# Two float32 products with 32 outputs on column quarters of TensorE, in place of depthwise products on 64x64 quarters

## The chip, the cores and the metric

The kernel runs on one core of one Trainium2 chip. The metric is the device time of the whole kernel in microseconds. In the profile, PE is TensorE's matmuls and PEld its weight loads, DVE is VectorE, ACT is ScalarE, POOL is GpSimd and SP is SyncE. A float32 matmul of the program stands in the trace as two records of PE and two of PEld, here called passes; a bf16 matmul is one of each.

## What is computed

The input x is 32 images of 96 channels, 56 x 56 pixels, float32. Two residual layers follow each other, each on the group-normalised input (`_gn`, 32 groups of three channels):

```
x = x + L0(gn(x))     # L0: 1x1 conv 96->576, BN, 4-bit activation;
                      #     3x3 depthwise conv on 576, BN, 4-bit activation;
                      #     1x1 conv 576->96, BN; plus its own input
x = x + L1(gn(x))     # L1, on three parts of 32 channels:
                      #   x_0 : 3x3 conv 32->32, weights gated per image
                      #   x_05: fractional Fourier transform (2D), 64x64 channel mix
                      #         gated per image, inverse transform, absolute value
                      #   x_1 : rfft2, 64x64 channel mix gated per image, irfft2
                      #   then a 3x3 conv 96->96 over the three results
```

The weights of L0 are quantised to 4 bits, so its weights and activations are small whole numbers, held exactly in bf16. L1 is computed in float32.

## The kernel before

**The loop.** Every image stays in SBUF as `x` (96 partitions x 3136). Layer 0 of image i and layer 1 of image i-1 are two lists of steps (lines 270 and 349), which `interleave` (line 76) merges in proportion to their lengths: 31 steps of layer 0 with 66 of layer 1. The tile framework then orders the instructions of each engine by this list and by its own estimate of when operands are ready, so that a few products move past others. Every engine works through its queue in that order.

**Layer 0** (lines 270 to 346) cuts an image into 8 chunks of 7 rows (392 pixels).

- `expand(j)` (282): VectorE normalises the chunk (v, line 285), TensorE multiplies it by w1 in five blocks of 128 hidden channels (pe, 288; the last block holds its 64 channels twice), and `quant_act` (257) makes 4-bit values: ScalarE Relu (260), VectorE twice (261, 265), into the padded bf16 planes q1.
- `depthwise(p, b)` (294): a depthwise 3x3 convolution as nine products with diagonal matrices. A diagonal of 64 channels is 64x64, so four products run side by side on the array's four 64x64 quarters: two halves of the block (h, rows) times two chunks of pixels (e, columns). The last block of 64 channels serves four chunks at once, in every second pair of chunks (line 341). Then `quant_act` into q2.
- `project(p)` (320): 72 paired products an image with w3 (pp, 324), then the residual (334) and the statistics for layer 1 (335).

In the list, five expands come first and the other three are put among the first depthwise steps (lines 338 to 345).

**Layer 1** (lines 349 to 609): `norm` (353) makes the statistics (helper `group_stats`, 237: pm, pv on TensorE, VectorE between), xs and x0p, and two DMAs on the SP queue copy x0p shifted by a row up and down, so that three rows of the spatial convolution lie on 96 partitions. Then come 7 transposes (pt, 439), the gates (pg, po; 374 to 384), forward_w (pf, 487), reflect (pr, 455), eight pairs of forward_h (pu, 497) and mix_f (pm, 515; it reads u, which VectorE and ScalarE make in lines 503 to 505), and:

- `mix_t` (558), 7 steps, one for each chunk of 8 rows (448 pixels): one float32 product with the gated weights g2, 128 inputs and 32 outputs (px, 560), for the first chunk a second one that adds the bias (564), and a copy into `cat` on VectorE (565);
- inverse_h (pi, 531), and `spatial` (567), 7 steps: three float32 products for dx = 0, 1, 2 with g0, 96 inputs and 32 outputs, into PSUM partitions 64 to 95 (ps, 570), and an activation into `cat` on ScalarE (578);
- inverse_w (pz, 544), `magnitude` (ScalarE, 553), `final` (580), the 3x3 convolution over `cat` as nine products for each of 7 chunks (pc, 584), and the store.

PSUM has two pools of four banks: ps0 for layer 0 (pe, pd, pp), ps1 for layer 1.

Of the kernel before, what the change touches and what calls it, by code (L numbers as in the profile page):

```python
# [44 lines left out]
NB = 5  # L46
NG64 = 9
# [18 lines left out]
NC0 = 8  # L66
CR0 = H // NC0
CN0 = CR0 * W
# [20 lines left out]
def block_kernel(ctx: ExitStack, tc: tile.TileContext, out: bass.AP, a: dict):  # L89
# [12 lines left out]
    def bank(pool, name):  # L102
        return pool.tile([128, 512], F32, tag="bank", name=name)
# [21 lines left out]
    with tc.tile_pool(name="prep", bufs=1) as pp:  # L125

        def load_tmp(name):
            src = a[name]
            t = pp.tile(list(src.shape), F32, tag=name, name=name)
            nc.scalar.dma_start(out=t, in_=src)  # L130
            return t
# [17 lines left out]
        quantise(w1, C, NB * 128, "1")  # L149
# [3 lines left out]
        quantise(w3f, 128, NG64 * C, "3")  # L153
        w3 = cp.tile([128, NG64 * C], BF16, tag="w3q", name="w3q")
# [4 lines left out]

        ident2 = pp.tile([128, 64], BF16, tag="ident2", name="ident2")  # L160
        nc.vector.tensor_tensor(ident2, ident[:, 0:64], ident[:, 64:128], ALU.add)
        dw = []
        for b in range(NB):
            d = cp.tile([128, 9, 64], BF16, tag=f"dw{b}", name=f"dw{b}")
            for t in range(9):
                nc.vector.tensor_scalar(d[:, t, :], ident2, w2[:, b * 9 + t : b * 9 + t + 1], None, ALU.mult)
            dw.append(d)
# [3 lines left out]
        v9 = load_tmp("vec9")  # L171
# [17 lines left out]
        A2, B2 = batchnorm(v9, 128, 0, NG64, "2")  # L189
# [67 lines left out]
    def quant_act(ps, k, scale, offset, dst, name):  # L257

        t = p4.tile([128, CN0], F32, tag="qt", name=f"qt{name}")
        nc.scalar.activation(t[:k], ps, AF.Relu, bias=offset, scale=scale)  # L260
        nc.vector.tensor_scalar(t[:k], t[:k], 15.0, MAGIC, ALU.min, ALU.add)  # L261
        src = t[:k]
        if len(dst.shape) == 3:
            src = src.rearrange("p (h w) -> p h w", w=W)
        nc.vector.tensor_scalar(dst, src, MAGIC, None, ALU.subtract)  # L265
# [4 lines left out]
    def layer0(i):  # L270
        xt = xts[i]
        s = {}

        def norm():
            stats = p2.tile([C, NCH, 6], F32, tag="bn", name=f"bn{i}")
            for j in range(NCH):
                nc.vector.bn_stats(stats[:, j, :], xt[:, j * CN : (j + 1) * CN])
            mean, rstd, _ = group_stats(stats.rearrange("p c s -> p (c s)"), f"a{i}")
            s["mean"], s["rstd"] = mean, rstd
            stats2[i] = p2.tile([C, NC0, 6], F32, tag="bn2", name=f"bn2{i}")  # L280

        def expand(j):
            part = xt[:, j * CN0 : (j + 1) * CN0]
            v = p2.tile([C, CN0], F32, tag="v", name=f"v{i}_{j}")
            nc.vector.tensor_scalar(v, part, s["mean"], s["rstd"], ALU.subtract, ALU.mult)
            for b in range(NB):
                ps = bank(ps0, f"pe{i}_{j}_{b}")
                nc.tensor.matmul(ps[:, :CN0], w1[:, 128 * b : 128 * (b + 1)], v, start=True, stop=True)  # L288
                dst = q1[b][:, 1 + CR0 * j : 1 + CR0 * (j + 1), 1 : 1 + W]
                quant_act(ps[:, :CN0], 128, A1[:, b : b + 1], B1[:, b : b + 1], dst, f"e{i}_{j}_{b}")  # L290

            nc.vector.scalar_tensor_tensor(part, part, B3, v, ALU.add, ALU.add)

        def depthwise(p, b):


            if b == 0:
                s["q2"] = s.pop("q2n", None) or p2.tile([128, NG64, CN0], BF16, tag="q2", name=f"q2_{i}_{p}")
            if b == NB - 1:
                s["q2n"] = p2.tile([128, NG64, CN0], BF16, tag="q2", name=f"q2_{i}_{p + 1}")  # L300
            pd = [bank(ps0, f"pd{i}_{p}_{b}_{h}") for h in range(2)]
            for t in range(9):
                dy, dx = divmod(t, 3)
                for h in range(2):
                    for e in range(2):
                        j = 2 * p + e + (2 * h if b == NB - 1 else 0)
                        nc.tensor.matmul(  # L307
                            pd[h][64 * e : 64 * e + 64, :CN0],
                            dw[b][64 * h : 64 * h + 64, t, :],
                            q1[b][64 * h : 64 * h + 64, CR0 * j + dy : CR0 * j + dy + CR0, dx : dx + W],  # L310
                            start=(t == 0),
                            stop=(t == 8),
                        )
            for h in range(2):
                g, q2 = (2 * b + h, s["q2"]) if b < NB - 1 else (NG64 - 1, s["q2n"] if h else s["q2"])
                quant_act(
                    pd[h][:, :CN0], 128, A2[:, g : g + 1], B2[:, g : g + 1], q2[:, g, :], f"d{i}_{p}_{b}_{h}"
                )

        def project(p):  # L320
            pp_ = [bank(ps0, f"pp{i}_{p}_{e}") for e in range(2)]
            for g in range(NG64):
                for e in range(2):
                    nc.tensor.matmul(  # L324
                        pp_[e][:C, :CN0],
                        w3[64 * e : 64 * e + 64, g * C : (g + 1) * C],
                        s["q2"][64 * e : 64 * e + 64, g, :],
                        start=(g == 0),
                        stop=(g == NG64 - 1),
                    )  # L330
            for e in range(2):
                j = 2 * p + e
                part = xt[:, j * CN0 : (j + 1) * CN0]
                nc.vector.scalar_tensor_tensor(part, pp_[e][:C, :CN0], A3, part, ALU.mult, ALU.add)
                nc.vector.bn_stats(stats2[i][:, j, :], part)

        ex = lambda j: (lambda: expand(j))
        steps = [norm] + [ex(j) for j in range(5)]
        for p in range(NC0 // 2):

            for b in range(NB - p % 2):
                steps.append(lambda p=p, b=b: depthwise(p, b))
                if (p, b) in ((0, 1), (0, 3), (1, 1)):
                    steps.append(ex({(0, 1): 5, (0, 3): 6, (1, 1): 7}[p, b]))
            steps.append(lambda p=p: project(p))
        return steps


    def layer1(i):
# [205 lines left out]
        def rows(j):  # L555
            return slice(1 + CR * j, 1 + CR * (j + 1))

        def mix_t(j):
            ps = bank(ps1, f"px{i}_{j}")
            nc.tensor.matmul(  # L560
                ps[:G, :CN], s["g2"], s["xs"][:, CR * j : CR * (j + 1), :], start=True, stop=(j > 0)
            )
            if j == 0:
                nc.tensor.matmul(ps[:G, :CN], bias2, pat, start=False, stop=True)
            nc.vector.tensor_copy(cat[:G, rows(j), 1 : 1 + W], ps[:G, :CN].rearrange("p (h w) -> p h w", w=W))

        def spatial(j):
            ps = bank(ps1, f"ps{i}_{j}")
            for dx in range(3):
                nc.tensor.matmul(  # L570
                    ps[2 * G : C, :CN],
                    s["g0"][:, G * dx : G * (dx + 1)],
                    x0p[:, CR * j : CR * (j + 1), dx : dx + W],
                    start=(dx == 0),
                    stop=(dx == 2),
                )
            src = ps[2 * G : C, :CN].rearrange("p (h w) -> p h w", w=W)
            nc.scalar.activation(cat[2 * G : C, rows(j), 1 : 1 + W], src, AF.Identity, bias=b0[2 * G : C], scale=1.0)  # L578
# [19 lines left out]
        def each(f, n):  # L598
            return [lambda k=k: f(k) for k in range(n)]
# [6 lines left out]
        steps += each(mix_t, NCH)  # L606
        steps += each(inverse_h, 4) + each(spatial, NCH) + each(inverse_w, 4) + [magnitude]
# [98 lines left out]
def _layout(inputs):  # L706
# [8 lines left out]
    def hidden(v):  # L715

        p = np.concatenate([v, v[HID - 64 :]])
        return np.moveaxis(p.reshape((NB, 128) + v.shape[1:]), 0, 1)

    def hidden64(v):  # L720

        p = np.moveaxis(v.reshape((NG64, 64) + v.shape[1:]), 0, 1)
        return np.concatenate([p, p])

    k["x"] = np.asarray(inputs["x"])
    w1 = g0("w1")[:, perm, 0, 0].T
    k["w1"] = np.concatenate([w1, w1[:, HID - 64 :]], axis=1)
    k["w2"] = hidden(g0("w2").reshape(HID, 9)).reshape(128, NB * 9)
    k["w3"] = hidden64(g0("w3")[perm, :, 0, 0].T).reshape(128, NG64 * C)
    names = ("b", "g", "be", "m", "v")  # L730
    k["vec576"] = np.stack([hidden(g0(n + "1")) for n in names], axis=1).reshape(128, 5 * NB)
    k["vec9"] = np.stack([hidden64(g0(n + "2")) for n in names], axis=1).reshape(128, 5 * NG64)
# [41 lines left out]
    k["b0"] = np.tile(g1("conv0_b"), 3)[:, None]  # L774
# [21 lines left out]
```

## Time and profile before

| | us |
|---|---|
| time, median of 2 runs (6797.88 and 6801.83) | 6799.85 |
| time of the profiled execution | 6797.88 |
| its span, first to last instruction | 6796.1 |
| mean granted clock of TensorE in it | 0.919 |
| PE busy (92% of the span) | 6275.5 |
| DVE busy (55%) | 3745.0 |
| ACT busy (38%) | 2558.7 |

The page's largest groups of TensorE (busy time, records): pc 1626.3 us in 4032, pe 1164.0 in 2560, pd 1048.2 in 20736, ps 538.7 in 1344, pr 357.1 in 2688, pp 224.6 in 2304, px 200.6 in 448 and 30.7 for its bias. Busy time is a union, so products that run side by side count once. Matmuls are pipelined: the time of one record on the page is longer than the distance of its start from the next one's, and distances are what adds up to the span.

### The profile page before, as it was taken

To read this page: it belongs to the slowest core of one execution; us is meant where nothing else is said; L and a number is where in the kernel's file an instruction comes from. 1 tells how busy PE (TensorE), PEld (TensorE's weight loads), DVE (VectorE), ACT (ScalarE), POOL (GpSimd) and SP (SyncE) were. 2 spreads that over 40 slices of the span, in tenths; PEclk is the share of its full clock that TensorE was granted. 3 is DMA by queue.
4 is the path that set the end of the run, shared out by engine and by line. 5 is a ranking of instruction groups with operands and counts; after the bars stand their busy time and mean duration, and the time that the engine had idled before them with its cause. 6 is when DMAs were issued, how large, how long until landed. Compare 5 with 4: busy or idle time off the path is not lost.

```text
span 6796.1 us, 114554 instructions
## 1 busy us (share of the span) xinstructions
PE 6275.5 (92%) x49088; PEld 3597.5 (53%) x49088; DVE 3745.0 (55%) x9182; ACT 2558.7 (38%) x4488; POOL 80.4 (1%) x114
## 2 busy tenths in 40 slices
PE   6999999999999999999999999999999999999998
PEld 3555555555555555455554555554555545555555
DVE  8466544565446665456654466544566544665442
ACT  4343333433334433344333343333443333433331
POOL 1000000000000000000000000000000000000000
PEclk9999999988999999999999999999999999999997
DMA  1000000000000000000000000000000000000000
GB/s 39 1 20 20 20 20 9 12 20 20 20 8 13 20 20 20 20 1 20 20 20 20 3 18 20 20 20 20 1 20 20 20 20 1 20 20 20 13 13 8
DMA packets 15982, 112.49 MB, mean 17 GB/s; under 512 B 6357, under 2 KB 6927, under 8 KB 7280
## 3 DMA queue, kind: packets, MB, share of 16 engines
q1 hardware_dynamic: 12288, 103.22, 6.8%
q8 instruction: 384, 6.29, 0.4%
q10 hardware_dynamic: 3184, 1.95, 0.1%
q14 instruction: 126, 1.03, 0.0%
HBM read 40.48 MB, written 38.54 MB: 12 GB/s over the span
## 4 chain that ended last, share of the span: by engine, by line
PE 76%; DVE 15%; ACT 7%; issue 1%; POOL 0%; DMA 0%; ACTq 0%; POOLq 0%; DVEq 0%
PE pc L584 24%; PE pe L288 14%; PE pd L307 10%; PE ps L570 8%; PE pr L455 5%; DVE q L265 4%; PE pi L531 3%; PE pm L515 2%; PE px L560 2%; DVE qte L261 2%; PE pp L324 2%; ACT cat L553 2%; ACT u L505 2%; ACT qte L260 2%; PE pu L497 2%; DVE u L504 1%
## 5 line engine op out<-in xcount | busy, mean ns | idle before, releaser
L584 PE MATMUL pc<-cat,wc 96*96 96x448 f32 x4032 | 1626.3, 563 | 102.1 <-ACT cat L553 102.1
L260 ACT ACTIVATE qte<-pe,o,s 128x392 f32<-128x392 f32 x1280 | 839.2, 677 | 1160.2 <-PE pe L288 1060.2
L260 ACT ACTIVATE qtd<-pd,o,s 128x392 f32<-128x392 f32 x1152 | 721.4, 674 | 1360.9 <-PE pd L307 1349.9
L288 PE MATMUL pe<-v,w 96*128 96x392 f32 x2560 | 1164.0, 608 | 54.2 <-DVE gtb L248 43.7
L584 PEld LDWEIGHTS pc<-cat,wc 96*96 96x96 f32 x4032 | 673.4, 170 | 1002.6 <-issue 888.3
L261 DVE TENSOR_SCALAR qtd<-qtd 128x392 f32<-128x392 f32 x1152 | 411.0, 359 | 1238.3 <-ACT qtd L260 1237.2
L307 PE MATMUL pd<-q,dw 64*64 64x392 bf16 x20736 | 1048.2, 339 | 0.6 <-ACT qte L260 0.3
L592 DVE SCALAR_TENSOR_TENSOR x<-pc,bc,x 96x448 f32<-96x448 f32 x224 | 152.3, 680 | 1286.7 <-PE pc L584 1286.7
L307 PEld LDWEIGHTS <-dw 64*64 64x64 bf16 x20736 | 649.8, 108 | 343.9 <-issue 161.0
L288 PEld LDWEIGHTS pe<-v,w 96*128 96x128 f32 x2560 | 570.3, 234 | 462.4 <-issue 238.6
L265 DVE TENSOR_SCALAR q<-qte 128x392 bf16<-128x392 f32 x1280 | 681.6, 555 | 10.9
L570 PE MATMUL ps<-x0p,g 96*32 96x448 f32 x1344 | 538.7, 549 | 0.0
L261 DVE TENSOR_SCALAR qte<-qte 128x392 f32<-128x392 f32 x1280 | 431.8, 355 | 92.2 <-ACT qte L260 84.2
L515 PE MATMUL pm<-g,u 128*57 128x64 f32 x3648 | 263.2, 225 | 199.1 <-ACT u L505 199.1
L265 DVE TENSOR_SCALAR q<-qtd 128x392 bf16<-128x392 f32 x1152 | 410.9, 359 | 25.7
L515 PEld LDWEIGHTS pm<-g,u 128*57 128x57 f32 x3648 | 226.7, 133 | 306.8 <-ACT u L505 289.5
L455 PEld LDWEIGHTS pr<-rev,X 56*128 56x128 f32 x2688 | 343.3, 206 | 38.1 <-DVE qte L261 17.1
L455 PE MATMUL pr<-rev,X 56*128 56x56 f32 x2688 | 357.1, 293 | 0.0
L570 PEld LDWEIGHTS ps<-x0p,g 96*32 96x32 f32 x1344 | 138.0, 110 | 330.5 <-issue 328.4
L505 ACT COPY u<-pu 32x456 f32<-32x456 f32 (+1 forms) x256 | 124.3, 486 | 439.9 <-DVE u L504 366.6
L467 ACT COPY xs<-pr 32x336 f32<-32x336 f32 (+3 forms) x448 | 183.1, 428 | 249.5 <-PE pr L455 135.1
L578 ACT ACTIVATE cat<-ps,b 32x448 f32<-32x448 f32 x224 | 140.6, 627 | 335.1 <-PE ps L570 335.1
(127 smaller groups left out, 5236.1 us busy)
## 6 DMA issues: line engine op xcount, KB each, us to landing
x<-in_x_dram SPq DMA_DIRECT2D x96, 392.0 KB, 5.4
out_dram<-x SPq DMA_DIRECT2D x96, 392.0 KB, 5.8
x0p<-x0p SPq DMA_DIRECT2D x64, 398.8 KB, 5.0
w<-in_w_dram ACTq DMA_DIRECT2D x1, 432.0 KB
wc<-in_wc_dram ACTq DMA_DIRECT2D x1, 324.0 KB
w<-in_w_dram ACTq DMA_DIRECT2D x1, 240.0 KB
cw<-in_cw_dram ACTq DMA_DIRECT2D x1, 128.0 KB
coef<-in_coef_dram ACTq DMA_DIRECT2D x1, 128.0 KB
```

What stands on the lines that cost most here:

```text
L260: nc.scalar.activation(t[:k], ps, AF.Relu, bias=offset, scale=scale)
L261: nc.vector.tensor_scalar(t[:k], t[:k], 15.0, MAGIC, ALU.min, ALU.add)
L265: nc.vector.tensor_scalar(dst, src, MAGIC, None, ALU.subtract)
L288: nc.tensor.matmul(ps[:, :CN0], w1[:, 128 * b : 128 * (b + 1)], v, start=True, stop=True)
L307: nc.tensor.matmul(pd[h][64 * e : 64 * e + 64, :CN0], dw[b][64 * h : 64 * h + 64, t, :], q1[b][64 * h : 64 * h + 64, CR0 * j + dy : CR0 * ...
L455: nc.tensor.matmul(ps[:, W * k : W * (k + 1)], lhs, rev[:, W * kind : W * (kind + 1)], start=True, stop=True)
L467: nc.scalar.copy(o, src)
L505: nc.scalar.copy(u[96:128, :n, :], U[:G])
L515: nc.tensor.matmul(ps[:L, 64 * k : 64 * k + 64], s["u"][:, k, :], s["g1"], start=True, stop=True)
L531: nc.tensor.matmul(ps[: 2 * L, H * k : H * (k + 1)], lhs, e57, start=True, stop=True)
L570: nc.tensor.matmul(ps[2 * G : C, :CN], s["g0"][:, G * dx : G * (dx + 1)], x0p[:, CR * j : CR * (j + 1), dx : dx + W], start=(dx == 0), sto ...
L584: nc.tensor.matmul(ps[:C, :CN], wc[:, C * t : C * (t + 1)], cat[:, CR * j + dy : CR * j + dy + CR, dx : dx + W], start=(t == 0), stop=(t = ...
```

## The change

Layer 0 goes over to 7 chunks of 8 rows, as in layer 1. The depthwise diagonals are 128x128 (64x64 in the last block), one product of 448 pixels after the other; the last block is no longer held twice; each chunk is projected with five products. The list of layer 0 becomes: norm, expand(0), and for each chunk j expand(j+1), five depthwise steps, project(j): 50 steps, merged with 56 of layer 1. In layer 1, `mix_t` and `spatial` take four chunks (the second time three) in one step: chunk e of the group goes to column quarter e of the array, that is, to PSUM partitions 32e to 32e+31 of one bank. The sums, the copies into `cat` and their number are the same.

```diff
-NC0 = 8
-CR0 = H // NC0
-CN0 = CR0 * W
+def blk(b):
+    return 128 if b < NB - 1 else HID - 128 * (NB - 1)
...
-            d = cp.tile([128, 9, 64], BF16, tag=f"dw{b}", name=f"dw{b}")
+            k = blk(b)
+            d = cp.tile([128, 9, 128], BF16, tag=f"dw{b}", name=f"dw{b}")
             for t in range(9):
-                nc.vector.tensor_scalar(d[:, t, :], ident2, w2[:, b * 9 + t : b * 9 + t + 1], None, ALU.mult)
+                nc.vector.tensor_scalar(d[:k, t, :k], ident[:k, :k], w2[:k, b * 9 + t : b * 9 + t + 1], None, ALU.mult)
...
-                nc.tensor.matmul(ps[:, :CN0], w1[:, 128 * b : 128 * (b + 1)], v, start=True, stop=True)
+                nc.tensor.matmul(ps[:k, :CN], w1[:, 128 * b : 128 * b + k], v, start=True, stop=True)
...
-        def depthwise(p, b):
...
-            pd = [bank(ps0, f"pd{i}_{p}_{b}_{h}") for h in range(2)]
+        def depthwise(j, b):
...
+            ps = bank(ps0, f"pd{i}_{j}_{b}")
             for t in range(9):
                 dy, dx = divmod(t, 3)
-                for h in range(2):
-                    for e in range(2):
-                        j = 2 * p + e + (2 * h if b == NB - 1 else 0)
-                        nc.tensor.matmul(
-                            pd[h][64 * e : 64 * e + 64, :CN0],
-                            dw[b][64 * h : 64 * h + 64, t, :],
-                            q1[b][64 * h : 64 * h + 64, CR0 * j + dy : CR0 * j + dy + CR0, dx : dx + W],
-                            start=(t == 0),
-                            stop=(t == 8),
-                        )
+                nc.tensor.matmul(
+                    ps[:k, :CN],
+                    dw[b][:k, t, :k],
+                    q1[b][:k, CR * j + dy : CR * j + dy + CR, dx : dx + W],
+                    start=(t == 0),
+                    stop=(t == 8),
                 )
...
+        def project(j):
+            ps = bank(ps0, f"pp{i}_{j}")
+            for b in range(NB):
+                k = blk(b)
+                nc.tensor.matmul(
+                    ps[:C, :CN], w3[:k, b * C : (b + 1) * C], s["q2"][:k, b, :], start=(b == 0), stop=(b == NB - 1)
+                )
...
+        steps = [norm, lambda: expand(0)]
+        for j in range(NCH):
+            if j + 1 < NCH:
+                steps.append(lambda j=j: expand(j + 1))
+            for b in range(NB):
+                steps.append(lambda j=j, b=b: depthwise(j, b))
+            steps.append(lambda j=j: project(j))
...
-        def mix_t(j):
-            ps = bank(ps1, f"px{i}_{j}")
-            nc.tensor.matmul(
-                ps[:G, :CN], s["g2"], s["xs"][:, CR * j : CR * (j + 1), :], start=True, stop=(j > 0)
-            )
-            if j == 0:
+        def mix_t(a):
+            ps = bank(ps1, f"px{i}_{a}")
+            quarters = [(e, 4 * a + e, ps[G * e : G * (e + 1), :CN]) for e in range(min(4, NCH - 4 * a))]
+            for e, j, o in quarters:
+                nc.tensor.matmul(o, s["g2"], s["xs"][:, CR * j : CR * (j + 1), :], start=True, stop=(j > 0))
+            if a == 0:
                 nc.tensor.matmul(ps[:G, :CN], bias2, pat, start=False, stop=True)
...
-        def spatial(j):
-            ps = bank(ps1, f"ps{i}_{j}")
+        def spatial(a):
+            ps = bank(ps1, f"ps{i}_{a}")
+            quarters = [(e, 4 * a + e, ps[G * e : G * (e + 1), :CN]) for e in range(min(4, NCH - 4 * a))]
             for dx in range(3):
-                nc.tensor.matmul(
-                    ps[2 * G : C, :CN],
-                    s["g0"][:, G * dx : G * (dx + 1)],
-                    x0p[:, CR * j : CR * (j + 1), dx : dx + W],
-                    start=(dx == 0),
-                    stop=(dx == 2),
+                for e, j, o in quarters:
+                    nc.tensor.matmul(
+                        o,
+                        s["g0"][:, G * dx : G * (dx + 1)],
+                        x0p[:, CR * j : CR * (j + 1), dx : dx + W],
+                        start=(dx == 0),
+                        stop=(dx == 2),
+                    )
...
-        steps += each(mix_t, NCH)
-        steps += each(inverse_h, 4) + each(spatial, NCH) + each(inverse_w, 4) + [magnitude]
+        steps += each(mix_t, 2)
+        steps += each(inverse_h, 4) + each(spatial, 2) + each(inverse_w, 4) + [magnitude]
```

The tensors on the host follow: w1 is 576 columns wide where it was 640, w3 480 where it was 864, the second batch normalisation shares the table of the first, and the spatial bias b0 is repeated four times. The evacuations of `mix_t` and `spatial` go over the quarters one by one, on the same engines as before.

## The prediction

> **What bounds the kernel now.** I read the page first: busy time, the clock row, the chain that ended last.
>
> ```profile
> span 6796.1 us, 114554 instructions
> ...
> PE 6275.5 (92%) x49088; PEld 3597.5 (53%) x49088; DVE 3745.0 (55%) x9182; ACT 2558.7 (38%) x4488; POOL 80.4 (1%) x114
> ...
> PEclk9999999988999999999999999999999999999997
> ...
> PE 76%; DVE 15%; ACT 7%; issue 1%; POOL 0%; DMA 0%; ACTq 0%; POOLq 0%; DVEq 0%
> ```
>
> PE holds 76% of the chain and is busy 92% of the span; no other engine passes 55%. The clock is below full almost everywhere. The first matmul (pma) of successive images starts 208.2 us apart, so I work on one image, 3071.7 to 3279.9 us, cut into stages in the view of windows: start, middle (reflections, forward, frequency mix), mix and inverse, spatial, final convolution.
>
> ```profile
> 3071.70:3110.70 39.00, 34.42 (x195) 20.44 (x194) 33.40 (x88) 21.03 (x37) 1.41 (x2) 0.82 0.38 84
> 3110.70:3167.50 56.80, 50.88 (x619) 39.14 (x617) 50.03 (x118) 31.16 (x60) 0.00 (x0) 0.94 0.01 2
> 3167.50:3191.10 23.60, 23.48 (x243) 13.69 (x242) 13.02 (x33) 7.26 (x12) 0.00 (x0) 0.93 0.00 1
> 3191.10:3225.00 33.90, 30.82 (x292) 14.15 (x291) 8.78 (x25) 16.54 (x25) 0.41 (x1) 0.99 0.00 1
> 3225.00:3279.90 54.90, 54.86 (x193) 23.67 (x194) 10.65 (x23) 3.74 (x6) 0.00 (x0) 0.95 0.00 0
> sum 208.20, PE 194.46 PEld 111.09 DVE 115.88 ACT 79.74 POOL 1.81; mean PE 38.89 PEld 22.22 DVE 23.18 ACT 15.95 POOL 0.36
> ```
>
> After each stage's length come PE, PEld, DVE, ACT and POOL busy, then the clock. PE idles 208.2 - 194.5 = 13.7 us. The clock takes, stage by stage, 39.0 x 0.18 + 56.8 x 0.06 + 23.6 x 0.07 + 33.9 x 0.01 + 54.9 x 0.05 = 15.2 us. PE work at full clock is the rest, 179.3 us. So 29 us of an image are idle time and slow clock: a change of order can give them back. In the first two stages VectorE is busy 83.4 of 95.8 us, near to being the bound.
>
> The timeline of PE gives the durations (start, time, what):
>
> ```profile
> 3191.11 2.44 PE L570 MATMUL ps<-x0p,g 96*32 96x448 f32 x6
> 3193.48 1.71 PE L307 MATMUL pd<-q,dw 64*64 64x392 bf16 x36
> 3195.11 4.70 PE L570 MATMUL ps<-x0p,g 96*32 96x448 f32 x12
> ...
> 3225.04 16.64 PE L584 MATMUL pc<-cat,wc 96*96 96x448 f32 x36 [3.12 <-ACT cat L553]
> 3241.61 0.85 PE L307 MATMUL pd<-q,dw 64*64 64x392 bf16 x13
> 3242.40 13.77 PE L584 MATMUL pc<-cat,wc 96*96 96x448 f32 x36
> ```
>
> A float32 matmul is two records (passes). 36 passes of the final convolution take 13.7 us, 381 ns each; the spatial product, with 32 of 128 columns in use, pays 395. One depthwise step (36 products, four at a time on the 64x64 quarters) takes 1.63 us. After 3.12 us of idleness 36 passes take 16.64 us.
>
> **What the Trainium skill says.** "TensorE: Matmul & The Clock Gate", Part 1: idle windows of about 3.4 us halve the clock. The trace agrees and shows more: a stretch without a gap, of small float32 products that wait for weight loads (reflections), halves it too (length, PE, clock):
>
> ```profile
> 3118.20:3121.60 3.40, 3.40 (x33) 1.00 0.00 0
> 3121.60:3128.40 6.80, 6.80 (x16) 0.50 0.00 0
> ```
>
> The same page, "Back-to-back issue gap", prices an N-column pass at N/2.4 + 2.5 ns. Part 3 there gives 2.38x for three column tiles and says that matmuls start in strict order. That matters: if the second pass of quarter 0 held back the first pass of quarter 1, only two passes would overlap. The trace contradicts it:
>
> ```profile
> 3110.50 0.41 PE L487 MATMUL pf<-e57t,X 56*56 56x57 f32 x4
> 3110.70 0.36 PE L307 MATMUL pd<-q,dw 64*64 64x392 bf16 x3
> 3110.75 0.26 PE L487 MATMUL pf<-e57t,X 56*56 56x57 f32 x2
> ```
>
> pf (56x56) fills the first 64x64 quarter and all of it is issued ahead of pd, yet three pd products start on the other quarters before its last two passes. Each tile of the array takes its own next instruction, so I expect four wide. "TensorEngine Tiling (Array Packing)", Key Properties: a change of tiling mode drains the array; the trace shows some 0.1 us at each (395 against 381 ns over six passes).
>
> **The change, PE work of one image at full clock.**
> - Depthwise: 4.5 x 4 = 18 steps of 1.64 us = 29.5 us go. 7 chunks x 5 blocks x 9 taps = 315 products of 448 bf16 columns come, the last block's 64x64 alone on the array. The trace has none of this form. Below: 189 ns by the page's price. Above: 182 ns x 448/392 = 208 ns, from the four-wide step with its four issues. I take 194: 187 ns plus the 7 ns by which a final pass exceeds 448 x 2 / 2.4 = 373. 61.1 us, **+31.6** (bounds +30.0 to +36.0). Weight loads (120 ns at most for 128 float32 columns, from the packed loads of the inverse) stay hidden under 194.
> - Spatial: 42 passes, 16.2 us by the timeline, become two groups of 6 slots: 12 x 0.40 + 0.2 = 5.0. **-11.2** (0 if serial).
> - Fourier mix: 14 passes and 2 for the bias, 6.7 us, become 4 + 2 slots (the bias follows in quarter 0 alone): 2.7. **-4.0**.
> - Expand: 80 passes of 392 columns at 334 ns become 70 of 448 at 381: 26.7 for 26.7. Project: 72 paired products, 6.5 us, become 35 at 194 ns: **+0.3**.
> - Mode changes: from 70 to 91 an image, as the small 64x64-mode products no longer share a mode with the depthwise ones: 21 x 0.1, part of it priced above: **+1.5**.
>
> Sum: 179.3 + 18.2 = **197.5 us**.
>
> *Idle time and clock.* Layer 0 goes from 31 coarse steps to 50, against 56 of layer 1, so a step of 1.7 us stands between nearly all small ones. In the new order pm has 10 to 19 depthwise products ahead of it where it now waits 5.9 us an image for u (ScalarE): 3 left. The final convolution waits 3.12 us for the magnitudes, after 2.7 us of cover; two blocks and a projection (5.4 us) come to stand there: 1 left. The gates' wait of 1.7: 0.5. The start keeps its 2.6 us, and gains: the last projection now comes just before the statistics, whose two VectorE operations (0.58 + 0.51 us, a little more at 448 columns) are no longer under a convolution, +1.3; the transposes wait for xs behind five products where eleven ran, +1. Sum 9.4, from 13.7. Slow clock: of five slow stretches (one of 3.4 us, four of 6.8) those at the gates, the reflections (now every other step dense) and the convolution should go; the start's stays (3.4 us lost), the inverse's half: 4.3, from 15.2.
>
> An image: 197.5 + 9.4 + 4.3 = **211.2 us**, +3.0; 31 images in the steady state: +93. The ends cancel roughly: the first image's layer 0, alone, has 94 us of PE work where it takes 81 now (+15 with its waits); the last image's layer 1, alone, saves what the two products cost there (10.1 + 19.0 to some 10, -19). 6796 + 93 is 6889 against the profiled execution's span; its time is 6797.9, the median 6799.9, so 2 to 4 us more: **6890**.
>
> What I cost at nothing: ScalarE gets the four spatial evacuations (627 ns each) in a burst after a bank is full, with expand's activations queued behind; a whole expand (3.8 us) on four other banks covers them, at most 2 us an image if not. VectorE's seven copies of the mix stay (606 ns). The x0p copies (SP queue, 5 us) are issued in the norm, 110 us ahead of their use; loads and stores keep their places. VectorE's layer 0 work is about the same, spread more evenly.
>
> **Rivals.**
> 1. *Two passes at a time* (order, or the moving data of four float32 streams; the trace has only two bf16 streams per row). Spatial takes 8.7 and mix 4.6: +5.6 an image, 7065. Against it: the pf/pd order above.
> 2. *The losses are not returned* (the slower side): a chunk's expand, five depthwise and projection form a chain through ScalarE and VectorE. If the start, with VectorE at 86%, stalls PE at each step, clock and gaps stay near 29 us: 226.4 an image, 7360; half returned, about 7130. It decides from 4.4 us an image over today's 208.2 (2% of 6800 over 31 images), that is, once 15 of the 29 us remain.
> 3. *More is returned*: no slow clock but at the start, gaps as short as 5 us: 205 to 206, 6720. Faster by 2% needs 203.8, total losses of 6.3 us, little more than the start alone.
> 4. *The quarters run serially*: +15.2, 7360.
>
> **Chances.** My forecast 0.47 (own range 6800 to 6960), rival 1 0.18, rival 2 0.16, rival 3 0.14, rival 4 0.05. Range 6700 to 7150: out are the full case of 2, all of 4 and the best of 3, some 0.19. Faster by over 2% (about what can be told from no change here): 0.07, half of 3. Slower: 0.42, from 1, 2, 4 and the upper end of mine. Same: 0.51.
>
> **What would show it.** ps in the new trace: 24 records in about 2.4 us (5 if two wide, over 9 if serial). pd: 194 ns start to start. PE's clock near 0.96, and full at the reflections and before the final convolution. I am wrong if pd's weight loads show (above 208 ns), if PE waits for q (VectorE) at depthwise or projection over 5 us an image, or if the start is slow for longer than 7 us.

## The result, and the profile after

The changed kernel takes 7528.1 us (median of 7525.35 and 7530.85) against 6799.85: 1.107 times as long, interval 1.102 to 1.112. The forecast was 6890, with a range to 7150. Times here are medians of runs in the chip's faster state; one run of pad_small (6938.9 us) fell into a slower one and is left out. The page of the changed kernel, with the lines that answer to those shown of before:

```profile
span 7529.1 us, 89648 instructions
...
PE 7341.6 (98%) x36928; PEld 3906.8 (52%) x36928; DVE 3598.2 (48%) x8669; ACT 2595.9 (34%) x4296; POOL 78.6 (1%) x114
...
PEclk9988899888988888988889888889888898888986
...
PE 96%; DVE 2%; ACT 1%; issue 1%; POOL 0%; DMA 0%; ACTq 0%; POOLq 0%
```

PE hardly waits now: it is 98% busy and holds 96% of the chain. But its granted clock has fallen from 0.919 to 0.875. So "PE is always busy" and "PE is slow" hold together. An image (first matmul pma to the next) takes 232 us in place of 208. The windows view of one of them (columns: stretch, length, busy PE, PEld, DVE, ACT and POOL, clock, DMA share, GB/s):

```profile
3631.60:3864.60 233.00, 229.74 (x1155) 120.80 (x1154) 111.82 (x268) 81.47 (x134) 1.76 (x3) 0.88 0.07 15
```

The only gaps that PE's timeline marks in that image are the two at its start:

```profile
3633.56 0.33 PE L244 MATMUL pva<-gta,gmat 96*96 96x1 f32 x2 [1.61 <-DVE gta L242]
...
3635.53 1.53 PE L283 MATMUL pe<-v,w 96*128 96x448 f32 x2 [1.48 <-DVE gtb L242]
```

The quarters run four wide, as the timeline shows for the two spatial groups of that image, the first at half clock and the second at full:

```profile
3780.74 4.71 PE L552 MATMUL ps<-x0p,g 96*32 96x448 f32 x24
3785.38 6.17 PE L283 MATMUL pe<-v,w 96*128 96x448 f32 x10
3791.48 2.46 PE L552 MATMUL ps<-x0p,g 96*32 96x448 f32 x18
3793.87 0.36 PE L296 MATMUL pd<-q,dw 128*128 128x448 bf16 x1
```

From the start of the 18 passes to the next product is 2.39 us: six slots of 398 ns. The 24 passes take 4.64 us, six slots of 773 ns, at the halved clock.

Three images from the middle of each trace give the account that the prediction made: gaps of PE over 0.1 us, half of the time at half clock, and the rest as work at full clock. The later rows are the experiments below. Over 29 images of each trace the mean time lies within 1.1 us of the one given here.

| kernel | us an image | work | gaps | lost to the clock |
|---|---|---|---|---|
| before | 208.2 | 179.2 | 13.7 | 15.4 |
| changed, as predicted | 211.2 | 197.5 | 9.4 | 4.3 |
| changed, as measured | 232.1 | 200.5 | 3.2 | **28.4** |
| last_rows | 223.0 | 200.5 | 3.2 | 19.3 |
| last_cols | 229.8 | 200.0 | 3.1 | 26.7 |
| serial | 242.3 | 217.1 | 3.1 | 22.2 |
| pad_small | 209.4 | 199.8 | 3.3 | 6.3 |
| pad_pe_pc | 222.3 | 201.4 | 3.2 | 17.6 |
| pad_all | 204.8 | 199.8 | 3.3 | 1.7 |
| both | 204.8 | 164.1 | 18.5 | 22.2 |
| both_pad | 198.0 | 164.5 | 21.6 | 11.9 |
| both_pad_order | 196.1 | 164.0 | 17.3 | 14.8 |
| before_pad | 202.7 | 180.6 | 15.9 | 6.3 |

Work is 3 us over the sum, gaps are 6 us under it, and the clock takes 24 us more than forecast. The miss of 21 us comes from the last column.

**Where the clock falls.** In the image above it is half for 13.65 us four times and for 3.41 us once. Its changes lie on a grid of 3.41 us; a window is one step of that grid. The windows around the third stretch (stretch, length, PE busy, clock, DMA share, GB/s), and PE's timeline of the same time:

```profile
3690.47:3693.88 3.41, 3.41 (x24) 1.00 0.00 0
3693.88:3697.29 3.41, 3.41 (x24) 1.00 0.02 5
3697.29:3710.94 13.65, 13.65 (x38) 0.50 0.00 0
```

```profile
3687.84 1.90 PE L296 MATMUL pd<-q,dw 128*128 128x448 bf16 x9
3689.67 1.54 PE L432 MATMUL pr<-rev,X 56*128 56x56 f32 x12
3691.14 1.90 PE L296 MATMUL pd<-q,dw 128*128 128x448 bf16 x9
3692.97 1.99 PE L432 MATMUL pr<-rev,X 56*128 56x56 f32 x16
3694.89 1.91 PE L296 MATMUL pd<-q,dw 64*64 64x448 bf16 x9
3696.73 1.68 PE L432 MATMUL pr<-rev,X 56*128 56x56 f32 x9
```

Both windows of 3.41 us have PE busy throughout and hold the same things: nine depthwise products and some 14 passes of pr. After the first the clock stays full, after the second it halves. What differs is that the nine products of the second are those of the last block: 64 rows x 64 columns, not 128 x 128. In streaming time, the time in which columns pass through the array, they are equal. At the prediction's price of 1/2.4 ns a column (twice that for a float32 pass), it is 9 x 187 ns + 14 x 47 ns = 2.34 us, 0.69 of the window. Weighted with the input rows in use, they are not: (1.68 + 0.66 x 56/128) / 3.41 = 0.58 against (1.68 x 64/128 + 0.66 x 56/128) / 3.41 = 0.33. Are rows what counts, or columns too? In the trace of before, a window holds nothing but the spatial product, 96 rows and 32 columns; the next stays at full clock:

```profile
3201.78 6.55 PE L570 MATMUL ps<-x0p,g 96*32 96x448 f32 x17
```

```profile
3203.53:3206.95 3.42, 3.42 (x10) 1.00 0.00 0
3206.95:3210.36 3.41, 3.41 (x42) 1.00 0.02 5
```

There rows x time is 0.75 and rows x columns 0.19 at most (the streaming fills about 0.95 of the window). So the theory for the experiments (R in the expectations): the clock is decided per window of 3.41 us by the time in which products stream, weighted with the input rows that they use. The rivals: T, streaming time alone, and C, rows x columns. That gaps alone decide it is out already: 13.7 us of gaps lose 15.4 us to the clock in the kernel before, 3.2 us lose 28.4 after.

The slow time of an image, put down to the stage in which a stretch begins (us at half clock, mean of 29 images; half of it is lost):

| kernel | start | gates | reflections | inverse | before the final convolution |
|---|---|---|---|---|---|
| before | 7.4 | 6.9 | 7.3 | 4.3 | 6.0 |
| changed | 9.9 | 13.5 | 22.7 | 11.3 | 0 |
| last_rows | 17.2 | 11.0 | 7.7 | 4.5 | 0 |
| last_cols | 7.6 | 13.9 | 15.2 | 16.7 | 0 |
| serial | 14.8 | 15.2 | 17.2 | 0 | 0 |
| pad_small | 6.8 | 6.9 | 0 | 0 | 0 |
| pad_pe_pc | 4.1 | 4.6 | 13.5 | 12.0 | 0 |

### The profile page after: what moved, and what is told of

It is laid out like the page before. It is cut to its first block, busy times and chain, and to the rows that moved or that the text cites. A ratio compares the mean times of both kernels' runs of the same rounds, so it can differ in the third digit from the quotient of the medians.

```text
span 7529.1 us, 89648 instructions
## 1 busy us (share of the span) xinstructions
PE 7341.6 (98%) x36928; PEld 3906.8 (52%) x36928; DVE 3598.2 (48%) x8669; ACT 2595.9 (34%) x4296; POOL 78.6 (1%) x114
## 4 chain that ended last, share of the span: by engine, by line
PE 96%; DVE 2%; ACT 1%; issue 1%; POOL 0%; DMA 0%; ACTq 0%; POOLq 0%
PE pd L296 28%; PE pc L569 20%; PE pe L283 16%; PE pr L432 6%; PE pp L309 4%; PE pi L508 4%; PE pm L492 3%; PE pu L474 3%; PE ps L552 3%; PE pf L464 2%; PE pt L416 2%; PE pz L521 1%; PE px L541 1%; PE pg L351 1%; PE po L358 1%
## 5 line engine op out<-in xcount | busy, mean ns | idle before, releaser
L296 PE MATMUL pd<-q,dw 128*128 128x448 bf16 (+1 forms) x10080 | 2244.5, 370 | 0.2 <-DVE q L259 0.2
L254 ACT ACTIVATE qtd<-pd,o,s 128x448 f32<-128x448 f32 (+1 forms) x1120 | 807.2, 723 | 2505.4 <-PE pd L296 2494.2
L296 PEld LDWEIGHTS <-dw 128*128 128x128 bf16 (+1 forms) x10080 | 964.3, 102 | 1014.6 <-issue 280.1
L283 PE MATMUL pe<-v,w 96*128 96x448 f32 (+1 forms) x2240 | 1308.5, 719 | 50.2 <-DVE gtb L242 44.6
L254 ACT ACTIVATE qte<-pe,o,s 128x448 f32<-128x448 f32 (+1 forms) x1120 | 786.0, 723 | 1035.0 <-PE pe L283 977.0
L255 DVE TENSOR_SCALAR qtd<-qtd 128x448 f32<-128x448 f32 (+1 forms) x1120 | 437.2, 390 | 1452.9 <-ACT qtd L254 1447.4
L283 PEld LDWEIGHTS pe<-v,w 96*128 96x128 f32 (+1 forms) x2240 | 452.3, 227 | 604.4 <-issue 347.8
L255 DVE TENSOR_SCALAR qte<-qte 128x448 f32<-128x448 f32 (+1 forms) x1120 | 422.4, 386 | 432.9 <-ACT qte L254 429.3
L259 DVE TENSOR_SCALAR q<-qtd 128x448 bf16<-128x448 f32 (+1 forms) x1120 | 432.4, 386 | 25.4
L259 DVE TENSOR_SCALAR q<-qte 128x448 bf16<-128x448 f32 (+1 forms) x1120 | 410.2, 388 | 8.5
```

What stands on the lines that cost most here:

```text
L283: nc.tensor.matmul(ps[:k, :CN], w1[:, 128 * b : 128 * b + k], v, start=True, stop=True)
L296: nc.tensor.matmul(ps[:k, :CN], dw[b][:k, t, :k], q1[b][:k, CR * j + dy : CR * j + dy + CR, dx : dx + W], start=(t == 0), stop=(t == 8),)
```

## The experiments

**last_rows**: the last block fed with 128 rows.

```diff
-                    dw[b][:k, t, :k],
-                    q1[b][:k, CR * j + dy : CR * j + dy + CR, dx : dx + W],
+                    dw[b][:, t, :k],
+                    q1[b][:, CR * j + dy : CR * j + dy + CR, dx : dx + W],
```

(w1's last block holds its channels twice, and both halves of its diagonals hold half of the weight.)

> The changed kernel, with the last depthwise block fed with 128 rows in place of 64 (its 64 channels stand twice, as in the kernel before, each copy with half the weight; 64 columns still). Instructions and their lengths are the same. Theory R (the clock of TensorE is halved after a window of 3.4 us in which time x input rows in use falls below about 0.38 of the full array, and comes back after a window above about 0.72): the slow stretches at the reflections and at the inverse, which begin after windows with this block in them (rows 0.32 and 0.34 by the trace), go; 27 to 31 of the 58 slow us of an image, 14 to 15 us gained, about 7080. Theory T (share of time with a product streaming, whatever its rows): nothing changes, 7530. Theory C (rows x columns in use): half of the gain, about 7300.

```profile
core 0: 7252.3 us, clock 0.907
```

Measured 7251.4 us, 1.066 times before (1.064 to 1.068): a gain of 277 us with the same work and the same gaps, against T. It is less than R's 450: the account shows 9 of the 14 to 15 us. At the reflections and the inverse the slow time falls from 34.0 to 12.2 us an image, most of what R says; but at the start, which this edit was not to touch, it grows from 9.9 to 17.2. What is left at the inverse begins, in one image, after a window that holds 26 passes of pi (57 rows) and part of a depthwise step, 0.36 by rows x time: two steps of pi lie together in the list and fill a window when it falls so. By its size alone this run does not part R from C.

**last_cols**: the last block written to 128 columns from 64 rows.

```diff
-                    ps[:k, :CN],
-                    dw[b][:k, t, :k],
+                    ps[:, :CN],
+                    dw[b][:k, t, :],
```

> The changed kernel, with the last depthwise block written to 128 columns in place of 64 (the second 64 repeat the first and are not read; 64 rows still). Theory R: no change, 7530 within 1%. Theory T: no change. Theory C: as with 128 rows and 64 columns, about 7300.

Measured 7424.3 us, 1.093 (1.091 to 1.096), 1.2% under the changed kernel's ratio: a little outside R's 1%. By its time alone it lies between R and C, with some 100 us gained where C forecast some 230. The stages part them. C makes the last block of last_cols and of last_rows equal, 64 rows x 128 columns and 128 x 64; yet at the reflections and the inverse 31.9 us an image are still slow here, against 34.0 in the changed kernel and 12.2 in last_rows. About half of the gain is at the start (9.9 to 7.6 us slow), which none of the theories forecast; that the windows fall otherwise on the steps is likely and not shown.

**serial**: the changed kernel with `mix_t` and `spatial` of the kernel before, chunk after chunk.

> The changed kernel with the two products with 32 outputs one chunk after the other as before (layer 0 of the changed kernel kept). If the quarters run four wide, 15.2 us of PE an image come back: 7528 + 32 x 15 = about 8010. If theory R holds the slow stretch after the inverse is shorter or as long, so not over 8100. If the quarters brought nothing: 7530.

Measured 7898.8 us, 1.162 (1.160 to 1.165), 110 us under the expectation. The quarters save 217.1 - 200.5 = 16.6 us of work there; 6.2 of them were lost to the clock. Without the quarters no slow stretch begins at the inverse (0 in place of 11.3 us). Whether that is the longer spatial product (96 rows for 12 us more) or the longer list, which lays the steps of layer 0 otherwise, is not shown.

**both**: the kernel before with only the quarters added.

```diff
-        steps += each(mix_t, NCH)
-        steps += each(inverse_h, 4) + each(spatial, NCH) + each(inverse_w, 4) + [magnitude]
+        steps += each(mix_t, 2)
+        steps += each(inverse_h, 4) + each(spatial, 2) + each(inverse_w, 4) + [magnitude]
```

> The kernel before with only the two products with 32 outputs moved to column quarters (its layer 0 on 64x64 quarters kept). Four wide: 15.2 us of PE an image less, 6800 - 32 x 15 = about 6320; 6320 to 6450 if the slow stretch at the inverse grows from 3.4 us. Were the quarters what slows the clock, it would stay near 6800 or above.

```profile
3196.50:3401.30 204.80, 186.33 (x1536) 0.89 0.08 17
```

Measured 6659.4 us, 0.980 (0.978 to 0.981), far short of 6320 to 6450. Work falls by 15.1 us, as priced, yet an image gains 3.4: gaps grow from 13.7 to 18.5 and the clock takes 22.2 in place of 15.4. The list of layer 1 is ten steps shorter, so the merge puts fewer steps of layer 0 between those that wait, and the spatial product no longer lends its rows; this reading was not tested by a run of its own.

**pad_small**: the changed kernel, the small float32 products pf, pr and pi on 128 rows. Nothing is added but rows: X and R lie in one tile of 128 partitions that is zeroed once, and the constants get rows of zeros.

```diff
-    k["e57"], k["e57t"] = e57, np.ascontiguousarray(e57.T)
+    k["e57"] = np.pad(e57, ((0, 128 - L), (0, 0)))
+    k["e57t"] = np.pad(e57.T, ((0, 128 - W), (0, 0)))
...
-                X = p1.tile([W, 2 * G * H], F32, tag="bigA", name=f"X{i}")
+                X = big["R"][:, : 2 * G * H]
```

> The changed kernel, with the small float32 products of the forward transform along the width, the reflections and the inverse along the height (56 or 57 input rows) run on 128 rows, the added rows zero in the weights side constants; same columns, so the same length of each. If the clock's meter counts rows addressed (theory R): the slow stretches at the reflections and the inverse go, as with the last block on 128 rows, 7050 to 7250. If it counts rows that carry data other than zero: no change, 7530. Theory T: 7530.

```profile
core 0: 6833.0 us, clock 0.962
```

```profile
3359.35 1.91 PE L301 MATMUL pd<-q,dw 64*64 64x448 bf16 x9
3361.18 1.54 PE L437 MATMUL pr<-rev,bigR 128*128 128x56 f32 x12
3362.57 0.92 PE L314 MATMUL pp<-q,w3q 128*96 128x448 bf16 x4
```

Measured 6834.8 us, 1.005 (1.004 to 1.007): some 690 us gone by multiplying zeros. The timeline shows the same place as above, now at full clock, though the last block is still on 64 rows; 12 passes of pr take 1.39 us to the next product, against 1.47 before the edit. The gain is larger than R's 7050 to 7250 allowed. No slow stretch begins at the reflections or the inverse any more. T gives no change, so T is out, and so is a meter that leaves out rows of zeros. So is the prediction's own account of the reflections, that their products wait for weight loads: these have as many columns as before. C is not put out by this run, since rows x columns grows with the rows too; the spatial window above and the pair last_rows and last_cols speak against C.

**pad_pe_pc**: expand and the final convolution on 128 rows, 32 of them zero.

```diff
-                nc.tensor.matmul(ps[:k, :CN], w1[:, 128 * b : 128 * b + k], v, start=True, stop=True)
+                nc.tensor.matmul(ps[:k, :CN], w1[:, 128 * b : 128 * b + k], vf, start=True, stop=True)
```

(vf is one of two tiles of 128 partitions, zeroed once; `cat`, wc and w1 get 32 rows of zeros.)

> The changed kernel, with expand and the final convolution on 128 input rows in place of 96, the added 32 rows zero. Theory R says that the slow clock ends after a window above about 0.72 of rows x time; expand at 96 rows gives 0.75 at most and reaches it in only some windows, on 128 rows in the first whole one: the stretches at the start, the gates, the reflections and the inverse start as before and end in 3.4 to 6.8 us in place of 13.7; 25 to 30 slow us an image fewer, about 7100. If zero rows do not count, or rows are not what is counted: 7530.

```profile
core 0: 7194.3 us, clock 0.919
```

Measured 7197.2 us, 1.059 (1.057 to 1.060), 100 us over the expected 7100. The slow stretches begin in the same stages. At the start and the gates most of them last 3.4 us, 4.1 and 4.6 in the mean in place of 9.9 and 13.5, as R says of the way back to full clock. At the reflections most still last 13.7, where no expand comes early.

**pad_all**: last_rows, pad_small and pad_pe_pc together.

> The changed kernel with all three: the last depthwise block, the small float32 products and expand and final on 128 rows. Work at full clock stays 200 us an image, gaps 3. Theory R: slow only at the start and perhaps the gates, 7 to 14 us, so 207 to 211 us an image and 6750 to 6900 in all, where the prediction had put the changed kernel. Theory T: 7530.

```profile
3227.20:3432.00 204.80, 201.44 (x1155) 0.99 0.07 17
```

Measured 6673.1 us, 0.981 (0.980 to 0.983): under R's 6750, and 1.9% under the kernel before. One slow stretch of 3.4 us is left, at the start. The account is 199.8 + 3.3 + 1.7.

**before_pad**: the kernel before with the zero rows of pad_small and pad_pe_pc.

> The kernel before, nothing changed but the rows of the small float32 products, expand and the final convolution filled up to 128 with zeros. Theory R: of its 31 slow us an image the stretches at the reflections and the inverse go and those after gaps (start, gates, final convolution) end in 3.4 us in place of 6.8: 7 to 14 us stay, 198 to 200 us an image in place of 208, 6480 to 6560. Theory T, or the clock following gaps alone: 6800, as work, gaps and lengths are the same.

```profile
3184.20:3386.20 202.00, 185.75 (x1535) 0.97 0.08 17
```

Measured 6612.2 us, 0.970 (0.969 to 0.972), short of R's 6480 to 6560: the clock gives back 9.1 us, gaps take 2.2 more and work 1.4. So the kernel before paid the same kind of toll, 15.4 us an image, with nothing in its busy time to show it.

**both_pad**: both packings with the zero rows.

> Layer 0 of the kernel before, the two products on column quarters, and the rows of the small float32 products, expand and final filled up to 128 with zeros. Theory R: of 44 slow us an image some 15 to 25 remain (gaps at the start, at the gates and before the final convolution start them, but they end sooner), 190 to 195 us an image, 6200 to 6350. Theory T: as without the zero rows, 6660.

Measured 6430.1 us, 0.945 (0.944 to 0.947), above R's 6200 to 6350 as the gaps did not shrink: 21.6 us an image, at the start, before the gates, before pm and before the final convolution.

**both_pad_order**: the same with another order of layer 1.

```diff
-        steps = [norm] + each(transpose, 7) + [gates]
-        steps += each(forward_w, 4)
+        steps = [norm] + each(transpose, 7) + each(forward_w, 4) + [gates]
...
-            steps += [lambda g=g: forward_h(g), lambda g=g: mix_f(g)]
+            steps += [lambda g=g: forward_h(g)] + ([lambda g=g: mix_f(g - 1)] if g else [])
+        steps += [lambda: mix_f(7)]
```

> Both packings with the zero rows, and the list of layer 1 in another order: the gates after the forward transform along the width in place of before it, and each frequency mix one step later, so that the next forward product stands between a product and its mix. The gaps ahead of pm (11 us an image in the kernel with both and zero rows) and ahead of the gates' first product (3.4) shrink to 2 to 5, and the slow stretches that they start go: 178 to 186 us an image in place of 198, 5820 to 6080. If the gaps only move elsewhere: 6430.

```profile
3126.90:3144.00 17.10, 15.80 (x69) 0.50 0.00 0
```

Measured 6385.7 us, 0.937 (0.936 to 0.939), the fastest of all, but 300 us over the expectation. The gaps ahead of pm went down from 9.2 to 4.0 us; a new one of 4.2 us came where expand waits for v, and the gates, moved, stand in about half of the images at the head of a slow stretch of 17.1 us (their products use 32 rows and one row). The gaps partly moved elsewhere.

## Why the prediction was wrong

**The step that failed** is "Slow clock: of five slow stretches ... those at the gates, the reflections (now every other step dense) and the convolution should go; the start's stays (3.4 us lost), the inverse's half: 4.3". Measured: 28.4 us. The stretch before the convolution went; the other four stayed or came back, and in the image shown each lasts 13.65 us where it lasted 6.83 or 3.41 (means of 29 images are in the table of stages). I had taken the clock for a matter of idle time and of products that wait for weight loads, so I counted every dense depthwise step as protection. It goes by rows x time. The trace of before held the signs: the reflections, without a gap, halved it, and the spatial product, with a quarter of the columns, did not. I read the first as an effect of weight loads and did not weigh the second. The idle windows of some 3.4 us that the prediction quotes from the Trainium skill are not what halves it here: in the changed kernel's image no gap is longer than 1.61 us, and the measurement decides.

Both halves of the change cost clock. The four kernels before, both, serial and changed are a square: the quarters alone raise the loss from 15.4 to 22.2 us, the new layer 0 alone (serial) also to 22.2, and together they raise it to 28.4. Why they make it worse is worked out here by the same measure, and only (1) and (2) were tested by edits (last_rows, pad_pe_pc): (1) before, a depthwise step kept all 128 rows at work in every block, since the last block served two row halves at once; now the last block's step counts half, and beside it the reflections (0.33) or the inverse (0.34) fall below the limit. (2) The way back needs a window above some 0.72. Before, after the start and the reflections at least ten passes of expand, 0.75 each, followed in a run; now transposes, pf and pr stand between them. In the image shown the first three windows of the long stretches come to 0.57 to 0.71 at the start, 0.48 to 0.68 at the gates and 0.18 to 0.56 at the reflections, so that a stretch lasts four windows. (3) The spatial product, 16 us at 0.75, shrinks to 5 us.

**Point by point.**
- *Depthwise*, 61.1 us at 194 ns: 63.2 by distances of starts in the changed kernel, weighted with the clock. Within a run (15 products in 2.88 us) it is 192 ns; the mode changes around each step, which I priced apart, make the rest. Weight loads stayed hidden.
- *Spatial* 5.0 and *mix* 2.7: 4.7 and 2.6. Four wide, right; the order of pf and pd in the trace of before was a sound ground. Rivals 1 and 4 fall.
- *Expand* 26.7: 29.0; *project* 6.8: 8.4. Both were priced too low, I think by the mode changes at their ends.
- *Gaps* 9.4: 3.2, as the finer list covers even the waits that I left in.
- *The ends*: 31 x (232.1 - 208.2) = 741 against a measured 733 of the spans; right within 8 us.
- Rival 2 named "clock and gaps stay near 29 us" and a time of 7360 with a chance of 0.16. The size of its loss is near (31.6), the mechanism is another: PE does not stall, it is slowed while busy.
- The signs: pd came at 192 ns and ps at 0.40 us a slot, six slots a group, as said. A clock near 0.96, full at the reflections, did not come, and the start was slow for longer than 7 us, which I had named as a sign of being wrong.

With the clock mended (pad_all), an image of the changed layer 0 takes 204.8 us, 6 under the forecast. The terms of the sum do not all hold there: work is 199.8 against 197.5, gaps are 3.3 against 9.4, and the gaps that I had put too long more than make up for the work that I had put too short. That part is luck.

## What to carry to other kernels

Before trusting a sum of PE times, mark the slow-clock windows in the trace and ask what each is preceded by, counting input rows x streaming time, not busy time. Where a product uses few of the 128 input rows, try filling them with zeros: in the changed kernel it cost no PE work (200.5 to 199.8 us an image) and kept the clock (some 690 us of 7528); in the kernel before it cost 1.4 us of work and 2.2 of gaps an image and still gained 5.5. A packing that saves PE time on a bound engine may take cover and clock from its neighbours: in the kernel before the quarters saved 15.1 us of work an image and gained 3.4, with the new layer 0 they saved 16.6 and gained 10.2.

## What the runs showed of the hardware that I had not expected

- Over five traces (before, changed, last_rows, last_cols, serial) the rule parts the windows of 3.41 us almost without exception. At full clock, below 0.36 of rows x time 607 of 609 are followed by half clock, above 0.42 none of 7713, between them 43 of 156. At half clock, below 0.67 none of 1288 is followed by full clock, above 0.74 428 of 436, between them 217 of 517. The seven other traces, from which the limits were not taken, agree: 818 of 820 and none of 10799 at full clock, 1 of 781 and 762 of 789 at half. (Each product counts with the streaming time of its columns, twice as long at half clock, times its rows / 128; products side by side on column tiles share that time.)
- The rivals do worse on the same windows. With the one limit that suits it best, rows x time puts 19 of the 8478 windows at full clock on the wrong side, streaming time alone 316 and rows x columns 362. With rows rounded up to whole 32 it is 21, to whole 64 it is 94. At half clock, rows and rows x columns do equally well in the five traces (102 and 100 wrong of 2241), and in the seven others rows do better (62 and 203 of 1704). How the chip measures it is not shown; rows of zeros count as rows (pad_small, pad_pe_pc).
- By the starts in the trace, a pass can go ahead of earlier passes of another tile of the array, in float32 too, where the Trainium skill, "TensorE: Matmul & The Clock Gate", Part 3, has matmuls in strict order: the eight passes of px on four quarters take 0.89 us to the next product, about two slots. The profile does not show the order of issue; if the two passes of a float32 product are issued one behind the other, strict order would let only two run at a time.
- The way down and the way back have different limits (some 0.37 and 0.71), so a stretch outlasts what began it. Products on 96 rows reach 0.75 at most and pass the upper limit only when they fill a window; on 128 rows (pad_pe_pc) most stretches at the start and the gates end after one window of 3.4 us.
